# A state-space block followed by an attention block on one core: the first batch's last norm, the key loads and the value projection are put in other places

## The chip, the cores and the metric

The kernel runs on one core of a Trainium2 chip. The core has five engines that run side by side, each taking its instructions in order: TensorE (PE) for matrix products, VectorE (DVE), ScalarE (ACT), GpSimd (POOL), and SyncE (SP), which here issues all DMA transfers. They wait for each other through semaphores. SBUF is the on-chip memory of 128 partitions; PSUM, eight banks of 2 KB per partition, takes what TensorE produces. GpSimd reads and writes SBUF, not PSUM, in this kernel.

The metric is the device time of one execution in microseconds (us).

## The reference

Two layers, for 2 batches of 2048 rows of 512 features, in float32:

```python
# layer 0: modulation by a condition vector, an S5 scan, a feed-forward part
y_mod = _ln(y) * (1 + scale_a[:, None]) + shift_a[:, None]
a_y = _s5(y_mod, ...)                      # complex diagonal recurrence along the rows
y = y + gate_a[:, None] * a_y
y_mod = (_ln(y) * (1 + scale_c) + shift_c) * (1 + scale_ff) + shift_ff
y = y + gate_ff[:, None] * (gelu(y_mod @ W1 + b1) @ W2 + b2)
# layer 1: attention with 16 heads of 32 features, a norm before and after
h = _sln(hidden, w, ...)                   # gamma * layernorm + beta, from the condition
q, k, v = split(h @ Wqkv.T + bqkv)
att = softmax(q @ k.T) / D ** 0.5
out = (att @ v) @ Wp.T + bp
h1 = out + hidden
return _sln(h1, w, ...) + h1
```

The last line is the "last norm" of the title: mean and variance of each row of `h1`, then a product with a row `g` of 512 values, plus a row `t`, plus `h1` itself.

## The kernel before

**First part, about 1380 us.** Each batch is cut into four chunks of 512 rows, eight in all (`order`). While one chunk goes through the feed-forward part, the next one is prepared and the one before is turned into keys, queries and values: `at_norm` (statistics, normalisation, the additions of the bias row on GpSimd, one write of the rows to DRAM as `x2`), `at_features` (transposes), `at_heads` (keys and queries, written as `kd`, `qd`), `at_values` (values, written as `vd`). What is left of this for the last two chunks stands in the list `left` and runs at the *seam*, while the attention starts. There `ones` has a single PSUM bank, so that each product must be emptied before the next one can start.

**Second part, the attention.** A *block* is one batch, one pair of heads and 512 queries: 2 x 8 x 4 = 64 blocks (`blocks`; the order of the last eight is changed). Each block takes NP = 8 *periods*; the main loop over `j` writes one period per round. Below, "period 5" is a round with `j` mod 8 = 5. For each block the 2048 keys are 16 tiles of 128, and the kernel works on two blocks at once:

- For the block AHEAD = 15 periods later it finds each query's maximum: `keep` computes the scores of tiles 0 to 9, copies them to SBUF with ScalarE and keeps a running maximum on VectorE (`run`; the first tile has none, and it falls in period 1); `across` computes the scores of tiles 10 to 15 the other way round (`m`) and reduces them on VectorE (`top`). Periods 0 and 4 keep two tiles, the others one.
- `turn_run` (periods 2 and 4) transposes the running maximum; `spread` (period 5) sends the negated maxima through DRAM (`flat`) back as a tile `shift` over all partitions.
- For the current block, `take_off` adds `shift` to kept tiles on GpSimd, one period before they are used and from period 7 of the block before on; `make` computes tiles 10 to 15 again and adds `shift` on VectorE (`pT`); ScalarE takes the exponentials; `weighted` multiplies with the values one period later.

Scores (`s`) have two PSUM tiles of two banks, `m` one of two banks, the output `o` one bank, and one bank, tag `pt`, is shared by `turn_run`, `spread`, the rows of the last norm, and the last norm's own tiles.

**Loads.** `load_k` loads the keys of a pair of heads with eight transfers of 256 KB, once every four blocks; `load_q` the queries of a block with eight of 64 KB, in period 3; `load_v` the values of a pair with two.

**The closing.** When a batch's heads are done, each tile of 128 queries (`qt`, 16 per batch) is *closed*: `fetch` (six transfers: the outputs, the divisors `by`, the rows `xr`), `divide` (GpSimd), `project` (product with `Wp`, one of its four groups per period for batch 0), `moments` (VectorE), `deviation` (VectorE: the inverse root by Newton steps on columns of one value per partition), `last_norm` (ScalarE, then the product with `g` on VectorE), `close` (GpSimd adds `t` and the rest; a write of the result). The 16 tiles of batch 0 are closed during the blocks of batch 1, in 16 of the blocks 34 to 57, those of batch 1 near the end.

The order is written out by hand: `after(j, what, ...)` puts a step at the start of period `j`, ahead of what the loop itself issues there, in the order in which the steps are listed. No scheduler moves anything. For batch 0's tile `qt`:

```python
k = NP * (NPAIR * NQ * (b + 1) + 2 + 3 * qt // 2) + 3
for g in range(NG):
    after(k + 3 + g, project, b, qt, (g,))
last = k + 6
after(k, fetch, b, qt)
after(k + 2, divide, b, qt)
after(last + 1, deviation, b, qt)
after(last + 2, last_norm, b, qt)
after(last + 3, close, b, qt)
```

In the loop, a period issues in this order: the steps that are due, `make`, `across`, the first exponential, `keep`, the pieces of `left`, the second exponential, `take_off`, `weighted`.

Of the kernel before, what the change touches and what calls it, by code (L numbers as in the profile page):

```python
# [19 lines left out]
P = 128  # L20
# [19 lines left out]
def tile_s5_block_then_sln_attention(  # L40
# [497 lines left out]
        nc.sync.dma_start(dst[0, g * P : (g + 1) * P, at], hi.bitcast(F32))  # L538
        nc.sync.dma_start(dst[1, g * P : (g + 1) * P, at], lo.bitcast(F32))

    def at_values(b, c, t):
        pv = ones.tile([P, CH], F32, name="pv")
        for k in range(KC):
            nc.tensor.matmul(
                pv, fts[b, c][:, k, t * P : (t + 1) * P], wv[:, k, :], start=k == 0, stop=k == KC - 1
            )
        vt = work1.tile([P, D], F32, name="vt", tag="gated")
        nc.vector.tensor_add(vt, pv, bv_row)
        nc.sync.dma_start(vd[b][c * CH + t * P : c * CH + (t + 1) * P, :], vt)


# [129 lines left out]
    left = []  # L681
    for chunk in order[-2:]:
        for t in range(TT):
            left.append((at_values, *chunk, t))
    for j in range(2 * KC):
        left.insert(TT + j, (at_heads, *order[-1], j))
    for k in range(KC):
# [206 lines left out]
    def project(b, qt, groups=tuple(range(NG))):  # L894

        o4, h, *py = held[b, qt]
        if py:
            py = py[0]
        elif len(groups) == NG:
            py = ps.tile([P, 2, CH], F32, name="py2", tag="m")[:, 0, :]  # L900
        else:
            py = ps.tile([P, CH], F32, name="py", tag="pt")
        for g in groups:
            nc.tensor.matmul(py, o4[:, g, :], wp[:, g, :], start=g == 0, stop=g == NG - 1)
        held[b, qt] = o4, h, py
        if groups[-1] == NG - 1:
            held[b, qt] = h, moments(h, py)

    def moments(h, py):
        nc.vector.tensor_add(h, py, h)  # L910
# [4 lines left out]
        return mv  # L915

    def deviation(b, qt):

        h, mv = held[b, qt]
        w = ps.tile([P, 3], F32, name="dev", tag="pt")  # L920
        v, c = w[:, 0:1], w[:, 1:2]
        half = small.tile([P, 1], F32, name="half3")
        y = small.tile([P, 1], F32, name="scale3", bufs=3)
        nc.vector.tensor_scalar(v, mv[:, 1:2], EPS, None, ALU.add)
        nc.vector.tensor_scalar(half, v, -0.5, None, ALU.mult)
        nc.vector.tensor_scalar(
            y.bitcast(I32), v.bitcast(I32), -0.5, float(0x5F3759DF), ALU.mult, ALU.add
        )
        for _ in range(3):
            nc.vector.tensor_scalar(c, y, y, half, ALU.mult, ALU.mult)  # L930
            nc.vector.scalar_tensor_tensor(y, c, 1.5, y, ALU.add, ALU.mult)
        shift = small.tile([P, 1], F32, name="shift3", bufs=3)
        nc.vector.tensor_scalar(c, mv[:, 0:1], y, None, ALU.mult)
        nc.vector.tensor_scalar(shift, c, -1.0, None, ALU.mult)
        held[b, qt] = h, y, shift

    def last_norm(b, qt):

        h, scale, shift = held[b, qt]
        z = ps.tile([P, CH], F32, name="z", tag="pt")  # L940
        nc.scalar.activation(z, h, AF.Identity, bias=shift, scale=scale)
        y = work.tile([P, D], F32, name="y")
        nc.vector.tensor_tensor(y, z, ending[b][0], ALU.mult)  # L943
        held[b, qt] = h, y

    def close(b, qt):

        h, y = held.pop((b, qt))
        nc.gpsimd.tensor_tensor(h, h, ending[b][1], ALU.add)  # L949
        nc.gpsimd.tensor_tensor(y, y, h, ALU.add)  # L950
        nc.sync.dma_start(out[b, qt * P : (qt + 1) * P, :], y)


# [98 lines left out]
    due = {}  # L1052

    def after(j, what, *args):
        due.setdefault(j, []).append((what, args))

    N = len(blocks)
    FIRST = -AHEAD - 8
    OPEN = -4
    for i, n in enumerate(opens):  # L1060
        free = NP * (max(m for m in range(N) if pair_of[m] == i - 2) + 1) if i > 1 else FIRST
        after(max(free, NP * n - AHEAD - 12), load_k, i)
        after(max(OPEN, NP * n - 9), load_v, i)
    for n in range(N):
        after(max(FIRST + 1 + n, NP * n - AHEAD - 6), load_q, n)
        after(NP * n - AHEAD + NP + 1, turn_run, n, 0)
# [2 lines left out]
    for b in range(NB):  # L1069
        for c in range(NQ):  # L1070
            j = NP * (blocks.index((b, NPAIR - 1, c)) + 1) + 1
            if (b, c) == (LB, LC):
                most = slice(0, NH - 4)
                j = NP * (N - 1) - 2
                after(j - 3, fetch_sums, b, c, most)
                after(j - 1, invert, b, c, most)
                after(j + 1, end_fetch)
                after(NP * (N - 1) + 3, end_fetch_more)
                for g in range(NG - 1):
                    after(j + 5 + g, end_divide, g)  # L1080
                after(NP * N + 2, end_project, list(range(NG - 1)))
                after(NP * N + 20, end_last)
                continue
            after(j, fetch_sums, b, c)
            after(j + 2, invert, b, c)
            if c == 0:
                after(j + 2, last_rows, b) if b == LB else after(NP * (NPAIR * NQ * (b + 1) + 2), last_rows, b)
            for t in range(TT):
                qt = c * TT + t
                if b == LB:  # L1090
                    k = j + 3 + 2 * t
                    after(k + 3, project, b, qt)
                else:

                    k = NP * (NPAIR * NQ * (b + 1) + 2 + 3 * qt // 2) + 3
                    for g in range(NG):
                        after(k + 3 + g, project, b, qt, (g,))
                last = k + 3 if b == LB else k + 6
                after(k, fetch, b, qt)
                after(k + 2, divide, b, qt)  # L1100
                after(last + 1, deviation, b, qt)
                after(last + 2, last_norm, b, qt)
                after(last + 3, close, b, qt)

    def run_due(j):
        for what, args in due.pop(j, ()):
# [6 lines left out]
    for j in range(FIRST, NP * N + 2):  # L1113
        if j == OPEN:
            assert not left
            late.close()
            fixed = ctx.enter_context(tc.tile_pool(name="fixed", bufs=1))
            kpools.append(ctx.enter_context(tc.tile_pool(name="kpool1", bufs=2)))
            ppool = ctx.enter_context(tc.tile_pool(name="ppool", bufs=2))
            rows = ctx.enter_context(tc.tile_pool(name="rows", bufs=2))  # L1120
            work = ctx.enter_context(tc.tile_pool(name="work2", bufs=2))
            ps_o = ctx.enter_context(tc.tile_pool(name="ps_o", bufs=1, space=PSUM))
            vst = [fixed.tile([P, NKT, 3, HD], F32, name=f"v{i}") for i in range(2)]
            for v in vst:
# [97 lines left out]
```

## Time and profile before

| | us |
|---|---|
| median of 3 runs | 3556.82 (3556.46 to 3561.1) |
| profiled execution, its own time | 3553.08 |
| its span | 3551.2 |
| PE busy | 3375.1 (95%) |
| DVE busy | 2243.7 (63%) |
| ACT busy | 1897.9 (53%) |
| POOL busy | 1977.0 (56%) |
| attention, batch 0 alone (2000 to 2520): PE busy | 507.12 of 520 |
| attention with closings of batch 0 (2600 to 3000): PE busy | 374.86 of 400 |

The profile is of one execution. "Busy" is the time in which an engine had an instruction; matrix products are pipelined, so a busy PE is not one at its peak. PEld is TensorE's weight load, which runs beside its products. In a line of the timeline the first number is the start in us from the beginning of the span, the second the duration, then the engine, the line of the kernel, the operation, the tiles written and read with their shapes, and in brackets the idle time of the engine just before, with what ended it. "SPq" is the queue that issues transfers. "x4" means four instructions of the kind in a row.

### The profile page before, as it was taken

The numbers are of one execution on the slowest core, as the hardware profiler recorded it, in microseconds if no ns is written. First come the engines' busy times: TensorE is split into PE (matmuls) and PEld (weight loads), VectorE is DVE, ScalarE is ACT, GpSimd is POOL, SyncE is SP. The second block draws the span as 40 slices with busy tenths as digits, with TensorE's granted clock in tenths as the row PEclk, the third lists the DMA queues.
The fourth block names the chain that finished last, engine by engine and source line by source line (L and its number), as shares of the span: only waits on it lengthen the run. The fifth ranks groups of instructions, "written<-read, shape, count | busy, mean of one in ns | idle before, by whom it ended". The sixth has DMA issues, their size and how long they took to land. (4 is left out here: it accounts for less than half of the span.)

```text
span 3551.2 us, 34223 instructions
## 1 busy us (share of the span) xinstructions
PE 3375.1 (95%) x11752; PEld 1531.9 (43%) x11752; DVE 2243.7 (63%) x3184; ACT 1897.9 (53%) x2143; POOL 1977.0 (56%) x1000
## 2 busy tenths in 40 slices
PE   7999999999999998899999999999999999999986
PEld 4444444444444443444444444444444444444432
DVE  6233232323222212589999999898888888988875
ACT  2111112111111111488888888888777877877853
POOL 4223131313131311288778888887777777777875
PEclk8999999999999999999999999999999999999998
DMA  8011111111101112412321222232323323323233
GB/s 296 1 36 39 45 42 48 36 48 36 54 33 39 36 45 74 119 47 64 76 69 49 71 65 70 49 75 61 87 67 81 82 69 77 76 72 88 59 94 98
DMA packets 201710, 237.07 MB, mean 67 GB/s; under 512 B 89857, under 2 KB 119041, under 8 KB 197441
## 3 DMA queue, kind: packets, MB, share of 16 engines
q1 hardware_dynamic: 201536, 234.89, 23.8%
q8 instruction: 93, 1.52, 0.2%
q14 instruction: 81, 0.66, 0.1%
HBM read 166.91 MB, written 67.76 MB: 66 GB/s over the span
## 5 line engine op out<-in xcount | busy, mean ns | idle before, releaser
L810 POOL TENSOR_TENSOR x<-x,shift 128x1024 f32<-128x1024 f32 x640 | 1505.1, 2391 | 284.1 <-DMA shift<-flat 237.6
L762 ACT COPY x<-s 128x1024 f32<-128x1024 f32 x640 | 635.2, 1013 | 297.7 <-PE s L751 294.2
L751 PE MATMUL s<-qs,ks 128*128 128x512 f32 x2048 | 699.5, 433 | 78.0 <-DVE run L767 55.9
L821 ACT ACTIVATE x<-x 128x1024 f32<-128x1024 f32 x640 | 676.4, 1057 | 42.8 <-POOL x L810 42.7
L767 DVE TENSOR_TENSOR run<-s,run 128x1024 f32<-128x1024 f32 x512 | 625.2, 1221 | 76.3 <-ACT x L762 57.4
L831 PE MATMUL o<-x,v 128*64 128x512 f32 x2560 | 669.5, 618 | 0.9 <-ACT x L821 0.9
L816 DVE TENSOR_TENSOR pT<-s,shift 128x1024 f32<-128x1024 f32 x384 | 467.4, 1217 | 49.8 <-PE s L751 44.2
L781 DVE TENSOR_REDUCE top<-m 128x1 f32<-128x768 f32 x512 | 485.9, 949 | 19.6 <-PE m L776 19.2
L751 PEld LDWEIGHTS s<-qs,ks 128*128 128x128 f32 x2048 | 347.4, 190 | 333.3 <-DVE run L767 144.7
L502 PE MATMUL po<-w_sb,hid 128*128 128x512 f32 x1024 | 460.3, 592 | 0.0
L489 PE MATMUL ph<-fT,w_sb 128*128 128x512 f32 x1024 | 459.7, 593 | 0.0
L821 ACT ACTIVATE pT<-pT 128x1024 f32<-128x1024 f32 x384 | 407.5, 1061 | 76.6 <-DVE pT L816 63.2
L493 ACT ACTIVATE hid<-ph,vec 128x512 f32<-128x512 f32 x128 | 88.0, 687 | 591.4 <-PE ph L489 591.4
L831 PE MATMUL o<-pT,v 128*64 128x512 f32 x1536 | 397.3, 596 | 4.6 <-ACT pT L821 4.6
L160 DVE SCALAR_TENSOR_TENSOR lo<-pk,vec,hi 128x512 fp32r<-128x512 f32 x64 | 48.0, 751 | 501.5 <-ACT hi L159 501.5
L776 PE MATMUL m<-ks,qs 128*128 128x384 f32 x1024 | 288.0, 362 | 7.0 <-DVE top L781 3.3
L489 PEld LDWEIGHTS ph<-fT,w_sb 128*128 128x128 f32 x1024 | 191.8, 190 | 226.5 <-issue 226.5
L502 PEld LDWEIGHTS po<-w_sb,hid 128*128 128x128 f32 x1024 | 191.1, 190 | 221.5 <-issue 221.5
L436 POOL TENSOR_TENSOR m<-m,m 128x512 f32<-128x512 f32 x8 | 13.1, 1643 | 442.1 <-DVE m L434 442.1
L159 ACT ACTIVATE hi<-pk,vec 128x512 fp32r<-128x512 f32 x64 | 44.0, 688 | 391.9 <-PE pk L532 391.9
L831 PEld LDWEIGHTS o<-x,v 128*64 128x64 f32 x2560 | 139.5, 136 | 263.6 <-issue 157.9
L512 POOL TENSOR_TENSOR x<-x,gated 128x512 f32<-128x512 f32 x32 | 39.6, 1271 | 349.5 <-DVE gated L511 349.5
(236 smaller groups left out, 2825.1 us busy)
## 6 DMA issues: line engine op xcount, KB each, us to landing
ks<-kd SPq DMA_DIRECT2D x128, 256.0 KB
qs<-qd SPq DMA_DIRECT2D x512, 64.0 KB
shift<-flat SPq DMA_DIRECT2D x64, 512.0 KB
x<-in_x SPq DMA_DIRECT2D x8, 1024.0 KB
w_sb<-in_w SPq DMA_DIRECT2D x8, 1024.0 KB
x<-x SPq DMA_DIRECT2D x8, 1024.0 KB
kd<-hi SPq DMA_DIRECT2D x32, 256.0 KB
kd<-lo SPq DMA_DIRECT2D x32, 256.0 KB
```

Of the source, the lines that this page charges most:

```text
L489: nc.tensor.matmul(ph, w1_sb[:, k, f * P : (f + 1) * P], fts[b, c][:, k, :], start=k == 0, stop=k == KC - 1)
L493: nc.scalar.activation(hids[f], ph, AF.Gelu_apprx_tanh, bias=vec[:, V_B1 + f : V_B1 + f + 1], scale=1.0)
L502: nc.tensor.matmul(pos[b, c][:, t, :], hid[:, t * P : (t + 1) * P], w2_sb[:, f, :], start=f == 0, stop=f == FC - 1,)
L751: nc.tensor.matmul(s[:, e, :], kst[pair_of[n], e][:, kt * P : (kt + 1) * P], qst[n][:, e, :], start=True, stop=True,)
L762: nc.scalar.copy(x, s)
L767: nc.vector.tensor_tensor(runs[n], s, kept[n, 0] if kt == 1 else runs[n], ALU.max)
L776: nc.tensor.matmul(m[:, i, :YW], qst[n][:, e, t * P : (t + 1) * P], kst[pair_of[n], e][:, k : k + YW], start=True, stop=True,)
L781: nc.vector.tensor_reduce(tops[n][:, j, 0:1], m[:, :, :YW], AX.XY, ALU.max, negate=True)
L810: nc.gpsimd.tensor_tensor(x, x, shifts[n], ALU.add)
L816: nc.vector.tensor_tensor(x, s, shifts[n], ALU.add)
L821: nc.scalar.activation(x, x, AF.Exp)
L831: nc.tensor.matmul(outs[n][64 * e : 64 * e + 64, :], v[:, kt, e : e + 2, :], x[:, e, :], start=first, stop=final,)
```

## The change

Five things, in the order of the code:

1. `at_values` gets a flag. With it, ScalarE copies the product from PSUM to SBUF and GpSimd adds the bias row there; without it, VectorE does both as before. It is set for the last chunk but one.
2. At the seam, the pieces of `left` in period -16 (the four `at_values` of the last chunk but one) are written ahead of `at_norm` of the last chunk, not behind it.
3. `moments` is a step of its own. For batch 0, `moments` and `deviation` go to the end of their period (`closing`, carried out behind the second exponential), not to its start.
4. The columns of `deviation` lie in SBUF (before: `v` and `c` in PSUM, bank `pt`); the second instruction of a Newton step is a `tensor_scalar` with the column as pointer, and one instruction makes `shift` where there were two. For batch 0, ScalarE writes the norm into SBUF, GpSimd multiplies with `g`, and `add_t` puts `h + t` into the tile that held the outputs; `fetch` comes two periods earlier, `last_norm` two and `close` three periods later.
5. `load_k` comes five periods later (period 2, before: period 5; the first one at -22 instead of -23), and the first `load_v` at -2 instead of -4.

```diff
-    def at_values(b, c, t):
+    def at_values(b, c, t, beside_norm=False):
...
-        nc.vector.tensor_add(vt, pv, bv_row)
+        if beside_norm:
+            nc.scalar.copy(vt, pv)
+            nc.gpsimd.tensor_tensor(vt, vt, bv_row, ALU.add)
+        else:
+            nc.vector.tensor_add(vt, pv, bv_row)
...
-            left.append((at_values, *chunk, t))
+            left.append((at_values, *chunk, t, chunk != order[-1]))
...
+    def add_t(b, qt):
+        h, ht, *_ = held[b, qt]
+        nc.gpsimd.tensor_tensor(ht, h, ending[b][1], ALU.add)
 
     def deviation(b, qt):
 
-        h, mv = held[b, qt]
-        w = ps.tile([P, 3], F32, name="dev", tag="pt")
-        v, c = w[:, 0:1], w[:, 1:2]
-        half = small.tile([P, 1], F32, name="half3")
+        h, ht, mv = held[b, qt]
+        v = small.tile([P, 1], F32, name="v3")
+        c = small.tile([P, 1], F32, name="c3")
         y = small.tile([P, 1], F32, name="scale3", bufs=3)
+        shift = small.tile([P, 1], F32, name="shift3", bufs=3)
         nc.vector.tensor_scalar(v, mv[:, 1:2], EPS, None, ALU.add)
-        nc.vector.tensor_scalar(half, v, -0.5, None, ALU.mult)
         nc.vector.tensor_scalar(
             y.bitcast(I32), v.bitcast(I32), -0.5, float(0x5F3759DF), ALU.mult, ALU.add
         )
+        nc.vector.tensor_scalar(v, v, -0.5, None, ALU.mult)
         for _ in range(3):
-            nc.vector.tensor_scalar(c, y, y, half, ALU.mult, ALU.mult)
-            nc.vector.scalar_tensor_tensor(y, c, 1.5, y, ALU.add, ALU.mult)
-        shift = small.tile([P, 1], F32, name="shift3", bufs=3)
-        nc.vector.tensor_scalar(c, mv[:, 0:1], y, None, ALU.mult)
-        nc.vector.tensor_scalar(shift, c, -1.0, None, ALU.mult)
+            nc.vector.tensor_scalar(c, y, y, v, ALU.mult, ALU.mult)
+            nc.vector.tensor_scalar(y, c, 1.5, y, ALU.add, ALU.mult)
+        nc.vector.tensor_scalar(shift, mv[:, 0:1], -1.0, y, ALU.mult, ALU.mult)
...
-        z = ps.tile([P, CH], F32, name="z", tag="pt")
-        nc.scalar.activation(z, h, AF.Identity, bias=shift, scale=scale)
...
-        nc.vector.tensor_tensor(y, z, ending[b][0], ALU.mult)
+        if b == LB:
+            z = ps.tile([P, CH], F32, name="z", tag="pt")
+            nc.scalar.activation(z, h, AF.Identity, bias=shift, scale=scale)
+            nc.vector.tensor_tensor(y, z, ending[b][0], ALU.mult)
+        else:
+            nc.scalar.activation(y, h, AF.Identity, bias=shift, scale=scale)
...
-        nc.gpsimd.tensor_tensor(h, h, ending[b][1], ALU.add)
-        nc.gpsimd.tensor_tensor(y, y, h, ALU.add)
+        if b == LB:
+            ht = h
+            nc.gpsimd.tensor_tensor(h, h, ending[b][1], ALU.add)
+        else:
+            nc.gpsimd.tensor_tensor(y, y, ending[b][0], ALU.mult)
+        nc.gpsimd.tensor_tensor(y, y, ht, ALU.add)
...
-        after(max(free, NP * n - AHEAD - 12), load_k, i)
-        after(max(OPEN, NP * n - 9), load_v, i)
+        after(max(free, NP * n - AHEAD - 7) if i > 1 else max(FIRST, NP * n - AHEAD - 7), load_k, i)
+        after(max(OPEN + 2, NP * n - 9), load_v, i)
...
+                    closing(k + 6, moments, b, qt)
                 last = k + 3 if b == LB else k + 6
-                after(k, fetch, b, qt)
+                after(k if b == LB else k - 2, fetch, b, qt)
                 after(k + 2, divide, b, qt)
-                after(last + 1, deviation, b, qt)
-                after(last + 2, last_norm, b, qt)
-                after(last + 3, close, b, qt)
+                (after if b == LB else closing)(last + 1, deviation, b, qt)
+                after(last + (2 if b == LB else 4), last_norm, b, qt)
+                after(last + (3 if b == LB else 6), close, b, qt)
+                if b != LB:
+                    after(last + 4, add_t, b, qt)
...
         if j == -AHEAD - 1:
-            at_norm(*order[-1])
             pieces = TT
...
             what(*args)
+        if j == -AHEAD - 1:
+            at_norm(*order[-1])
         if now is not None:
             exponentials(now, uses[k][1])
+        run_due(j + 0.5)
```

More of the change, by code (lines that the diff above doesn't have):

```diff
@@ L905, in project, with moments @@
         held[b, qt] = o4, h, py
-        if groups[-1] == NG - 1:
-            held[b, qt] = h, moments(h, py)
-    def moments(h, py):
+    def moments(b, qt):
+        o4, h, py = held[b, qt]
         nc.vector.tensor_add(h, py, h)
@@ L914, in moments @@
         nc.vector.bn_aggr(mv, st)
-        return mv
+        held[b, qt] = h, o4.rearrange("p g q -> p (g q)"), mv
+    def add_t(b, qt):
+        h, ht, *_ = held[b, qt]
+        nc.gpsimd.tensor_tensor(ht, h, ending[b][1], ALU.add)
     def deviation(b, qt):
-        h, mv = held[b, qt]
-        w = ps.tile([P, 3], F32, name="dev", tag="pt")
-        v, c = w[:, 0:1], w[:, 1:2]
-        half = small.tile([P, 1], F32, name="half3")
+        h, ht, mv = held[b, qt]
+        v = small.tile([P, 1], F32, name="v3")
+        c = small.tile([P, 1], F32, name="c3")
         y = small.tile([P, 1], F32, name="scale3", bufs=3)
+        shift = small.tile([P, 1], F32, name="shift3", bufs=3)
         nc.vector.tensor_scalar(v, mv[:, 1:2], EPS, None, ALU.add)
-        nc.vector.tensor_scalar(half, v, -0.5, None, ALU.mult)
         nc.vector.tensor_scalar(
@@ L928, in deviation @@
         )
+        nc.vector.tensor_scalar(v, v, -0.5, None, ALU.mult)
         for _ in range(3):
-            nc.vector.tensor_scalar(c, y, y, half, ALU.mult, ALU.mult)
-            nc.vector.scalar_tensor_tensor(y, c, 1.5, y, ALU.add, ALU.mult)
-        shift = small.tile([P, 1], F32, name="shift3", bufs=3)
-        nc.vector.tensor_scalar(c, mv[:, 0:1], y, None, ALU.mult)
-        nc.vector.tensor_scalar(shift, c, -1.0, None, ALU.mult)
-        held[b, qt] = h, y, shift
+            nc.vector.tensor_scalar(c, y, y, v, ALU.mult, ALU.mult)
+            nc.vector.tensor_scalar(y, c, 1.5, y, ALU.add, ALU.mult)
+        nc.vector.tensor_scalar(shift, mv[:, 0:1], -1.0, y, ALU.mult, ALU.mult)
+        held[b, qt] = h, ht, y, shift
     def last_norm(b, qt):
-        h, scale, shift = held[b, qt]
-        z = ps.tile([P, CH], F32, name="z", tag="pt")
-        nc.scalar.activation(z, h, AF.Identity, bias=shift, scale=scale)
+        h, ht, scale, shift = held[b, qt]
         y = work.tile([P, D], F32, name="y")
-        nc.vector.tensor_tensor(y, z, ending[b][0], ALU.mult)
-        held[b, qt] = h, y
-    def close(b, qt):
-        h, y = held.pop((b, qt))
-        nc.gpsimd.tensor_tensor(h, h, ending[b][1], ALU.add)
-        nc.gpsimd.tensor_tensor(y, y, h, ALU.add)
+        if b == LB:
[4 more added lines that the diff above has]
+            nc.scalar.activation(y, h, AF.Identity, bias=shift, scale=scale)
+        held[b, qt] = h, ht, y
+    def close(b, qt):
+        h, ht, y = held.pop((b, qt))
+        if b == LB:
[4 more added lines that the diff above has]
+        nc.gpsimd.tensor_tensor(y, y, ht, ALU.add)
         nc.sync.dma_start(out[b, qt * P : (qt + 1) * P, :], y)
@@ L1055, in after, with closing @@
         due.setdefault(j, []).append((what, args))
+    def closing(j, what, *args):
+        due.setdefault(j + 0.5, []).append((what, args))
     N = len(blocks)
@@ L1092, in tile_s5_block_then_sln_attention @@
                     after(k + 3, project, b, qt)
+                    after(k + 3, moments, b, qt)
                 else:
```

## The prediction

> **What bounds the kernel now.** The table of waits says who waits for whom, but its sums mix stages. I therefore read busy times by stage, and marked in the timeline each period's first matmul on `m` (L776), which cuts the attention into periods. In the columns below, "x" counts instructions; after the engines come the granted clock, the DMA share and GB/s. The first row is a block of batch 0, the second a block of batch 1 with one closing of batch 0.
>
> ```profile
> core 0: us, PE busy (x) PEld busy (x) DVE busy (x) ACT busy (x) POOL busy (x), PEclk, DMA share, GB/s
> 2390.77:2419.55 28.78, 28.24 (x123) 12.84 (x122) 26.36 (x28) 25.71 (x29) 23.71 (x11) 1.00 0.16 44
> 2620.06:2654.23 34.17, 32.07 (x130) 14.20 (x129) 30.05 (x42) 26.74 (x30) 27.23 (x14) 1.00 0.37 81
> ```
>
> An undisturbed block takes 28.8 us with TensorE (PE) busy 98%. Its eight intervals, from period 1 to 2 on, are 4.25, 3.35, 3.20, 4.00, 3.87, 3.35, 2.78, 4.01 us. The 27 blocks from 2419.55 take 120 us more than that, and the excess repeats to 0.02 us: each closing's four matmul groups add 0.85, 0.86, 0.56 and 1.05 (3.32, PE's own work), its deviation, norm and close -0.51, 1.56, 0.87, 0.14 (2.06). Five times the third of these is some 1.5 larger, at half clock. The rest is late shifts.
>
> Before the attention comes the seam (timeline):
>
> ```profile
> 1380.57 3.60 PE L544 MATMUL pv<-wv,fT 128*128 128x512 f32 x8
> 1390.79 3.81 DVE L143 TENSOR_SCALAR xn<-x,mean,rstd 128x512 f32<-128x512 f32 x4
> 1394.52 0.68 DVE L548 TENSOR_TENSOR vt<-pv,bv_row 128x512 f32<-128x512 f32 x1
> 1395.26 5.51 PE L544 MATMUL pv<-wv,fT 128*128 128x512 f32 x8 [11.09 <-DVE vt L548]
> 1409.17 0.91 PE L776 MATMUL m<-ks,qs 128*128 128x384 f32 x2
> ```
>
> The first `pv` is done at 1384.2, but VectorE (DVE) empties it only after `at_norm`'s whole statistics and normalisation. PE stands 11.1 us and then runs eight matmuls at two thirds of its clock (5.51 us for 3.60).
>
> Late shifts, an undisturbed one first (timeline):
>
> ```profile
> 2405.70 0.27 SPq L802 DMA_DIRECT2D flat<-neg_row  x1
> 2410.82 2.40 POOL L810 TENSOR_TENSOR x<-x,shift 128x1024 f32<-128x1024 f32 x1 [5.07 <-DMA shift<-flat]
> ...
> 2434.48 0.27 SPq L802 DMA_DIRECT2D flat<-neg_row  x1
> 2440.41 0.35 SPq L804 DMA_DIRECT2D shift<-flat  x1
> 2444.35 11.72 POOL L810 TENSOR_TENSOR x<-x,shift 128x1024 f32<-128x1024 f32 x5 [10.01 <-DMA shift<-flat]
> 2450.04 1.06 PE L751 MATMUL s<-qs,ks 128*128 128x512 f32 x2 [2.29 <-DVE run L767]
> ```
>
> GpSimd (POOL) can start 5.1 us after `flat` is issued, but 9.9 us when `load_k`'s eight transfers (from 2428.4) were issued in the same period 5.
>
> A closing (timeline):
>
> ```profile
> 2654.10 0.68 DVE L910 TENSOR_TENSOR xr<-py,xr 128x512 f32<-128x512 f32 x1
> 2655.65 1.21 DVE L816 TENSOR_TENSOR pT<-s,shift 128x1024 f32<-128x1024 f32 x1
> 2658.43 0.16 DVE L924 TENSOR_SCALAR dev<-mv 128x1 f32<-128x1 f32 x1
> 2660.66 0.16 DVE L934 TENSOR_SCALAR shift<-dev 128x1 f32<-128x1 f32 x1
> 2662.01 0.74 PE L751 MATMUL s<-qs,ks 128*128 128x512 f32 x2 [1.20 <-DVE pT L816]
> 2663.87 0.68 DVE L943 TENSOR_TENSOR y<-z,g_row 128x512 f32<-128x512 f32 x1
> 2670.53 0.73 PE L751 MATMUL s<-qs,ks 128*128 128x512 f32 x2
> ```
>
> DVE runs without a gap from 2654.10 to 2671.72, and PE waits for it.
>
> **The Trainium skill.** "SBUF — State Buffer", section "Who interferes with whom", says that DVE and GpSimd share one port pair under an exclusive lock: a DVE instruction with two SBUF inputs, or in a two-port mode, waits out a GpSimd one. "VectorE: DVE Perf Modes", section "What auto-detection actually checks", gives that mode to an SBUF-to-SBUF instruction with one source whose outermost sizes are even or equal; a column of one element might count. The trace agrees on wide tiles, not on a column (timeline):
>
> ```profile
> 158.39 1.71 POOL L462 TENSOR_TENSOR xn<-xn,r_scale 128x512 f32<-128x512 f32 x1
> 159.01 0.21 DVE L454 COPY last<-m 128x1 f32<-128x1 f32 x2
> ...
> 3540.36 1.73 DVE L1026 TENSOR_TENSOR o<-o,h 128x512 f32<-128x512 f32 x1 [1.16 <-POOL h L1024]
> ```
>
> The last takes 0.69 without GpSimd; the column copies don't wait for the 1.71. "TensorE: Matmul & The Clock Gate", Part 1, lets idle windows halve the clock; here it was 0.60 in 2525.5 to 2529.6, after waits.
>
> **The change part by part.**
>
> *Values at the seam.* The four `at_values` now precede `at_norm`, with ScalarE emptying PSUM (a 128x512 copy: 0.59, from `raw`). Before, `pv` starts 4.49 apart (1401.55, 1406.04); with the shorter copy 4.4. The second pays some 1.1 more, because the first copy's buffer is held by GpSimd's third `gated` addition (to 1385.3). So `m` starts at 1380.57 + 3 x 4.4 + 1.1 + 3.2 = 1398.1 instead of 1409.17: -11. `at_norm` ends on DVE at 1394.6, hidden behind these matmuls. On GpSimd the four additions of `bv_row` (1.27 each) come ahead of `at_norm`'s; on SP the four `vd` writes come ahead of the `x2` write, to about 1405, before the heads' writes behind it. If these writes were held up: at most 5. I take -10.8.
>
> *First v load.* It moves behind the first shift on SP. That shift needed 8.3 us from `flat` (1480.00 to 1488.28); at 5.2 GpSimd is done with its first tile at 1487.6, then the table load (to 1488.6) decides: the first exponential at 1488.65 instead of 1490.67, -2.0. `v` is issued some 4 us later and first needed some 12 us after that; if it doesn't land in time, up to +3.
>
> *Keys.* Issued in period 2, three periods (10.6 us) ahead of the next `flat`; the transfers take some 10. The first use stays seven periods (25 us) away. They pass `load_q` (period 3) on SP, whose queries are needed later. Six blocks of batch 1 lose: 3.30, 5.65, 5.00, 1.37, 3.49, 4.67, sum 23.5. In batch 0 the same lateness (up to 7.8 us from `flat`) cost PE nothing, so 2 us of remaining overlap cost nothing either. I take -23.5; bounds -25 and -12.
>
> *Closings of batch 0, 16 times.* Removed from DVE: the product with g (0.60 until the next starts). Deviation: 2.31 from 2658.43 to `pT`. After: ten instructions; a plain one is spaced 0.19, one pointer adds 0.06 (L933: 222 against 158 ns), two 0.12 (L930: 281). So 4 x 0.19 + 0.06 (shift) + 3 x (0.32 + 0.25) = 2.5. The moments (1.55) stood in a gap that the last `py` group makes; now they follow period 1's `top`, where an undisturbed block has a gap of 1.28 (no running maximum in that period), but `pT` starts only at 2654.44, when its `s` is there. DVE's chain then ends at 2654.44 + (17.62 - 1.55 - 2.31 - 0.60 + 1.55 + 2.5) = 2671.65 against 2671.72. The wait moves: `py` keeps the bank that the transposes of the running maximum need until 2657.2 (0.25), and late is not the third scores tile but the `m` of period 4, behind `top` (1.7). I take -0.07 x 16 = -1, bounds -16 and +10. Longer single waits may bring two more half-clock spells: +2.
> ScalarE gains nothing: the norm moves to period 5, where it idles 0.66 for 0.80 of work. GpSimd's product is 1.28 more per closing, in period 7; there it waits 1.5 to 2.9 us for the shift anyway, and no longer stands 5 us for z; without that cover 20. `fetch` two periods earlier (six DMAs, past `load_q`) ends GpSimd's waits for `by` (43 us), which were hidden.
>
> *Batch 1's deviation*, 12 times 0.2 us longer but out of the shared bank: 0, bounds -3 and +3.
>
> Sum: -10.8 - 2.0 - 23.5 - 1 + 2 = -35.3. The profiled execution took 3553.1 (span 3551.2), 3.7 below the median of the runs; 3556.8 - 35.3 = **3521.5**.
>
> **Rivals.** *Keys only half freed* (chance 0.15): the burst with the queries behind it still reaches `flat`; half the 23.5 remains: 3533. For it: 2.5 MB in 11 us. Against: a late shift up to 7.8 us was free. *The closings' wait vanishes* (0.17): PE's own outputs of the previous period cover the deviation, 1.5 of the 2.06 goes: 3521.5 - 23 - 3 = 3496. Against: DVE has no gap there. *Columns take the port lock* (0.05), the case that ends slower: each of ten column instructions waits out a 2.39 us GpSimd tile, on average half, 12 us a closing, 28 closings: some 3850. It decides from 35/28 = 1.3 us per closing. Against: the column copies above.
>
> **How the numbers follow.** The forecast's case has 0.63. Its own range, from seam (2), keys (4) and closings (10), is 3509 to 3534; with the rivals at 3496 and 3533, 3495 to 3536. A measurement here tells 0.2% (7 us) from no change: faster 0.93, same 0.02, slower 0.05.
>
> **What would show it.** `m` first at about 1398; 5.1 us from `flat` to GpSimd in every fourth block; closings still adding some 5.3 us, with PE waiting at period 4's `m`; column instructions at 0.15 to 0.28 us. Wrong if these stretch, or if late shifts stay.

## The result and the profile after

The changed kernel takes 3513.66 us (median of 4 runs, 3509.6 to 3514.7). The kernel before took 3556.64 beside it. The ratio is 0.9878, with a 95% interval of 0.9861 to 0.9895. The profiled execution went from 3553.08 to 3509.6, -43.5 us, where the forecast had -35.3. The sum came out 8 us off, but two of its terms were wrong by more than that, in opposite directions.

Marking each period's first matmul on `m` again (now L780) cuts both executions into the same stages:

| us | before | after | difference |
|---|---|---|---|
| seam: first `pv` to first `m` | 28.60 | 17.35 | -11.25 |
| first `m` to the third block (`j` = 17) | 146.27 | 146.40 | +0.13 |
| batch 0's blocks, `j` = 17 to 257 | 864.11 | 863.87 | -0.24 |
| blocks with batch 0's closings, `j` = 257 to 473 | 898.07 | 869.97 | -28.10 |
| `j` = 481 to the end | 204.77 | 200.49 | -4.28 |

The busy times of an undisturbed block and of a block with one closing, after the change (columns as in the forecast's first view):

```profile
core 0: us, PE busy (x) PEld busy (x) DVE busy (x) ACT busy (x) POOL busy (x), PEclk, DMA share, GB/s
2379.67:2408.47 28.80, 28.27 (x123) 12.85 (x121) 26.38 (x28) 25.71 (x29) 23.50 (x11) 1.00 0.14 44
2501.51:2535.28 33.77, 32.21 (x131) 14.29 (x130) 29.43 (x39) 26.64 (x30) 29.24 (x15) 1.00 0.25 67
```

An undisturbed block is what it was. The block with a closing takes 5.0 us more: 3.31 for the four matmul groups, which is PE's own work, and 1.65 for the rest of the closing (before 2.06).

The seam (timeline):

```profile
1385.57 0.59 ACT L549 COPY vt<-pv 128x512 f32<-128x512 f32 x1 [10.64 <-POOL x L512]
...
1398.20 0.91 PE L780 MATMUL m<-ks,qs 128*128 128x384 f32 x2
...
1416.98 0.75 DVE L160 SCALAR_TENSOR_TENSOR lo<-pk,vec,hi 128x512 fp32r<-128x512 f32 x1 [5.58 <-DMA kd<-lo]
```

ScalarE empties the first `pv` as soon as GpSimd has released the buffer, PE no longer stands 11 us behind `at_norm`, and the products come 4.4 us apart (5.4 the first time). `m` starts at 1398.20, where the forecast had 1398.1. The last line is the price. On SP the write of `x2` waits for the norm until 1405.72, and the eight query transfers behind it go right ahead of the heads' first write. That write, issued at 1411.73, takes 5 us to land, and its tile can be rewritten only then. Period -12 is 1.06 longer for it (0.4 to 1.4 in the nine kernels here that have this seam).

A closing (timeline):

```profile
2643.32 0.15 DVE L932 TENSOR_SCALAR v<-mv 128x1 f32<-128x1 f32 x1
...
2643.48 4.70 POOL L814 TENSOR_TENSOR x<-x,shift 128x1024 f32<-128x1024 f32 x2
...
2643.88 0.27 DVE L938 TENSOR_SCALAR c<-scale,v 128x1 f32<-128x1 f32 x1
...
2645.68 1.22 DVE L820 TENSOR_TENSOR pT<-s,shift 128x1024 f32<-128x1024 f32 x1
...
2647.82 0.62 PE L780 MATMUL m<-ks,qs 128*128 128x384 f32 x2 [1.17 <-DVE top L785]
```

The ten column instructions take 2.36 us from 2643.32 to the next `pT`. GpSimd works on two tiles all that time, and none of the ten is stretched (0.15, 0.21 or 0.27 us by the number of columns that an instruction takes as pointers). PE now waits once, at the `m` of period 4. Before, it waited 1.20 at `s` behind `pT` (the prediction shows that line) and two us later 0.51 behind `run` (timeline of the kernel before):

```profile
2664.01 0.73 PE L751 MATMUL s<-qs,ks 128*128 128x512 f32 x2 [0.51 <-DVE run L767]
```

The late shifts are not gone. In block 37 (timeline; "SPq" issues transfers in order):

```profile
2570.26 1.22 SPq L890 DMA_DIRECT2D xr<-x  x1
2571.52 7.77 SPq L733 DMA_DIRECT2D ks<-kd  x8
2580.34 8.10 SPq L743 DMA_DIRECT2D qs<-qd  x8
2588.53 0.27 SPq L806 DMA_DIRECT2D flat<-neg_row  x1
...
2594.28 11.64 POOL L814 TENSOR_TENSOR x<-x,shift 128x1024 f32<-128x1024 f32 x5 [10.32 <-DMA shift<-flat]
...
2599.93 0.74 PE L755 MATMUL s<-qs,ks 128*128 128x512 f32 x2 [2.39 <-DVE run L771]
```

`neg_row`, which `flat` sends, is ready at 2580.63 (ScalarE's copy, 2580.39 to 2580.63). `flat` is issued at 2588.53, 7.9 us later, because SP has still to issue the queries. Those take 3.6 to 3.9 us for eight transfers when little is under way (before, at 2588.56 and 2552.57), and 8.1 here, behind 2 MB of keys, which themselves took 7.8 behind the six transfers of `fetch`. From `flat` to GpSimd it is 5.75 us (5.1 undisturbed), so the transfer itself is hardly late. In block 33, which has keys and no fetch, the queries take 8.4 us too, but begin five us after the keys, and `flat` goes out only 0.7 us late. In the five blocks where keys and fetch meet (37, 41, 49, 53, 56) `flat` goes out 5.9 to 7.9 us late, and the end of the block and the start of the next lose 4.35, 1.05, 2.56, 1.34 and 0.46 us, 9.8 in all. Before, it was 23.5 in six other blocks.

### The profile page after: what moved, and what is told of

Read it like the earlier page. It is cut to its first block, busy times and chain, and to the rows that moved or that the text cites. A ratio compares the mean times of both kernels' runs of the same rounds, so it can differ in the third digit from the quotient of the medians.

```text
span 3507.7 us, 34138 instructions
## 1 busy us (share of the span) xinstructions
PE 3362.0 (96%) x11752; PEld 1526.4 (44%) x11752; DVE 2229.1 (64%) x3136; ACT 1897.0 (54%) x2147; POOL 1997.6 (57%) x1020
## 5 line engine op out<-in xcount | busy, mean ns | idle before, releaser
L780 PE MATMUL m<-ks,qs 128*128 128x384 f32 x1024 | 284.8, 359 | 23.7 <-DVE top L785 22.1
```

The source lines that it names most:

```text
L780: nc.tensor.matmul(m[:, i, :YW], qst[n][:, e, t * P : (t + 1) * P], kst[pair_of[n], e][:, k : k + YW], start=True, stop=True,)
```

## The experiments

Each kernel is compared with the kernel before, which took 3555.6, 3556.8 and 3557.9 us in the three groups. The stage "closings' blocks" is `j` = 257 to 473 of the profiled execution. What a block or a closing "loses" or "costs" is the sum of what its periods took over those of an undisturbed block; a closing's matmul groups are left out. A "spell" is a stretch at half clock in a closing. A late shift is named by the block in which its `flat` is issued.

### Which part brings what: three parts alone

**Seam alone**: `at_values` ahead of `at_norm` with ScalarE and GpSimd, and the first `load_v` at `OPEN + 2`.

> The kernel before with the seam alone changed (values ahead of the norm, emptied by ScalarE; first load of v two periods later). Theory of the forecast: the first m at about 1398.1 instead of 1409.2 and period 0 two us shorter, together -12.8 us, so 3544. What the traces of the two kernels suggest: -10.9 at the first m, +1.0 lost again some three periods later, -2.0 in period 0, +1.0 in period 1 where the values now come late: -10.9 in all, 3546. In both the later blocks stay as they were before.

Measured 3538.84, ratio 0.996 (0.9945 to 0.9975). The stage from `pv` to `m` is 17.35 and the next one 146.48, just as in the changed kernel: -11 us from the seam. Periods -1 to 1, around the first use of `v`, take 14.68 and not 15.63. Up to `j` = 17 this comes to 11 us, but the medians differ by 16.8. In the profiled executions the rest lies in the closings' blocks, whose code is the same: 889.94 us against 898.07, with 2 spells against 5 and 19.7 us of late shifts against 23.5. So much can differ there with nothing changed in the stage; whether by chance or by the earlier start was not shown.

**Keys alone**:

```diff
-        after(max(free, NP * n - AHEAD - 12), load_k, i)
+        after(max(free, NP * n - AHEAD - 7) if i > 1 else max(FIRST, NP * n - AHEAD - 7), load_k, i)
```

> The kernel before with the loads of the keys alone moved to period 2. Theory of the forecast (the late shifts were the keys' transfers, and they are gone): -23.5 us, 3533. Theory from the trace after (the eight key transfers fill SP's queue; the queries behind them are issued in 8 us and not in 4, and flat, which is behind the queries, goes out late where the six transfers of fetch come in the same block): the six old stalls go, new ones of 1 to 3 us each come at the end of blocks 37, 41, 49, 53 and 56, so -10 to -17, 3540 to 3547. Here fetch is still in period 3, behind the queries, so the new stalls may be longer than in the changed kernel.

Measured 3557.16, ratio 1.0011 (1.0003 to 1.0018); closings' blocks 904.75, 6.7 more than before. Both theories fall. All six old stalls are gone, as both had said. But blocks 37, 41, 49, 53 and 56 lose 8.3, 4.5, 8.2, 5.2 and 5.1 us in periods 5 and 6, at a place that neither had named. There PE waits for the first group of `py`, by 6.17 us in block 37. It waits for GpSimd's division, and the division for `by` (timeline). `fetch` is still in period 3 and stands behind keys and queries.

```profile
2605.94 1.26 POOL L891 TENSOR_TENSOR o<-o,by 128x512 f32<-128x512 f32 x1 [13.16 <-DMA by<-invd]
...
2607.25 2.08 PE L904 MATMUL py<-wp,o 128*128 128x512 f32 x2 [6.17 <-POOL o L891]
```

**Closings alone**: items 3 and 4 of the change, `fetch` and `close` included, with seam and keys as before.

> The kernel before with the closings alone changed (moments and deviation at the end of their periods, columns in SBUF, product with g on GpSimd, fetch two periods earlier); keys and seam as before. Theory of the forecast: -1 from VectorE's chain and +2 from spells of half clock, so no change, 3557 to 3558. Theory from the trace after: 1.65 us a closing instead of 2.06, 16 times, -6.6; and the five closings that lost 1.5 more at half clock lose it no longer, -7: 3543. The late shifts of the keys stay in both, and with fetch earlier they may even be shorter.

Measured 3526.79, ratio 0.9925 (0.991 to 0.994): -29 us, twice what I expected. The closings' blocks take 867.70, which is 2.3 *less* than in the changed kernel with its moved keys. Each closing costs 1.65, none runs at half clock, and with the keys still in period 5 the late shifts shrank from 23.5 to some 8 us. So something in the closings' part frees the shifts, and no gain in this stage is left for the move of the keys. The 2.3 us themselves say little, since late shifts differ by more than that between executions (19.7 and 23.5 above).

### What in the closings' part freed the shifts

**Fetch alone, two periods earlier, in the kernel before**:

```diff
-                after(k, fetch, b, qt)
+                after(k if b == LB else k - 2, fetch, b, qt)
```

> The kernel before with one step alone moved: fetch of batch 0's tiles two periods earlier (period 1 and not 3). Theory of SP's queue: before, the fetch of period 3 stands right ahead of the keys of period 5 and of flat; ahead of them by four periods, it no longer does, and most of the late shifts go although the keys stay in their place: -12 to -16 of the 23.5 us, and with fewer long waits also some half-clock spells of 1.5 each: 3535 to 3543. Theory of the forecast (the fetch is hidden, the late shifts are the keys' alone): no change, 3555.

Measured 3552.64, ratio 0.9987 (0.9979 to 0.9996). My theory falls: blocks 32, 36, 40, 44, 48 and 52 still lose 3.1, 6.1, 4.2, 1.4, 5.7 and 4.1 us at their end and the start of the next block, 24.6 in all, as before. In block 40 the last of the keys are still issued just ahead of `flat`, and `shift` follows `flat` by 8.2 us (7.4 in the kernel before).

**Close alone, three periods later, in the kernel before**:

```diff
-                after(last + 3, close, b, qt)
+                after(last + (3 if b == LB else 6), close, b, qt)
```

> The kernel before with one step alone moved: close of batch 0's tiles three periods later (period 7 and not 4), fetch and keys in their old places. Theory of SP's queue, second form: the write of the result, which waits on SP for GpSimd's sums in period 4, holds the keys behind it until some 4 us before flat; without it in front they go 7 us earlier, and the late shifts of blocks 36, 44 and 48 (5.65, 1.37 and 3.49) go, those of 32, 40 and 52 stay: -9 to -10.5, 3546. Rival (the moved close does nothing for SP; the late shifts shrank by less work on VectorE): no change, 3556.

Measured 3549.04, ratio 0.9971 (0.9961 to 0.9982). Blocks 36 and 48 lose nothing any more and block 44 0.26; 32, 40 and 52 still lose 3.5, 5.1 and 6.6. The timeline of SP in block 36, first of the kernel before:

```profile
2552.57 3.86 SPq L739 DMA_DIRECT2D qs<-qd  x8
2563.63 0.36 SPq L951 DMA_DIRECT2D out<-y  x1
2564.03 3.68 SPq L729 DMA_DIRECT2D ks<-kd  x8
2568.26 0.27 SPq L802 DMA_DIRECT2D flat<-neg_row  x1
2576.05 0.34 SPq L804 DMA_DIRECT2D shift<-flat  x1
```

and of the kernel with the later close:

```profile
2557.03 3.90 SPq L739 DMA_DIRECT2D qs<-qd  x8
2560.97 3.67 SPq L729 DMA_DIRECT2D ks<-kd  x8
2572.70 0.27 SPq L802 DMA_DIRECT2D flat<-neg_row  x1
2573.97 0.34 SPq L804 DMA_DIRECT2D shift<-flat  x1
```

In the kernel before, the write of the result stands ahead of the keys in SP's order and waits for GpSimd's sums until 2563.63, with SP idle for seven us. The keys are ready to go all that time, and when they go they are 4.2 us ahead of `flat`. Without the write in front they follow the queries at once, 11.7 us ahead of `flat`, and `shift` follows `flat` by 1.3 us and not by 7.8. In these blocks it was a *waiting* transfer on SP that brought the keys so close to `flat`. Blocks 40 and 52 have no `close`. They lose 5.1 and 6.6 here, 4.2 and 4.1 with `fetch` alone moved, and 1.7 and 2.0 with the whole closings' part; what does that was not taken apart.

### The fetch in the changed kernel, and the keys at a better place

**Fetch back to period 3 in the changed kernel** (the diff of the fetch above, reversed):

> The changed kernel with fetch alone back in its old place (period 3, behind the queries). Theory: as in the kernel with the keys alone moved, the fetch stands behind the keys and the queries in blocks 37, 41, 49, 53 and 56, the division comes late, and the first group of the product waits in TensorE's order: 4 to 8 us each, less the 10 us of late shifts that go with it, +20 to +25: 3534 to 3539. Theory of the forecast (fetch is hidden wherever it stands): 3514.

Measured 3535.53, ratio 0.9938 (0.9918 to 0.9957), as the theory said; closings' blocks 896.11, 26.1 more. Block 37 in the timeline:

```profile
2570.06 8.49 SPq L743 DMA_DIRECT2D qs<-qd  x8
2578.59 0.42 SPq L882 DMA_DIRECT2D o<-od  x1
2579.06 1.93 SPq L886 DMA_DIRECT2D by<-invd  x4
...
2587.38 1.26 POOL L895 TENSOR_TENSOR o<-o,by 128x512 f32<-128x512 f32 x1 [11.92 <-DMA by<-invd]
...
2588.69 2.08 PE L908 MATMUL py<-wp,o 128*128 128x512 f32 x2 [6.32 <-POOL o L895]
```

The division waits 11.9 us for the divisors, and PE then 6.3 for the division. So the earlier fetch, worth at most some 4 us alone, is what makes the keys in period 2 bearable.

**Keys in period 6 in the changed kernel**, behind `flat` and `shift`:

```diff
-        after(max(free, NP * n - AHEAD - 7) if i > 1 else max(FIRST, NP * n - AHEAD - 7), load_k, i)
+        after((max(free, NP * n - AHEAD - 11) if i > 1 else NP * n - AHEAD - 11) if i else FIRST + 1, load_k, i)
```

> The changed kernel with the loads of the keys moved once more, to period 6, so that they are issued behind flat and shift and not ahead of them. Theory of SP's queue: in no block does flat stand behind the keys; the stalls at the end of blocks 37, 41, 49, 53 and 56 (2.67, 0.65, 2.15, 0.93, 0.05, with 1.68, 0.40, 0.41, 0.41, 0.40 at the start of the block behind each) are gone, -9 to -10 us: 3504. Rival, the bandwidth of the transfers: 2 MB right behind the shift delay the shift itself as they did before the change (9.9 us from flat to GpSimd), and the time goes back towards 3535.

Measured 3503.79, ratio 0.9859 (0.9844 to 0.9874); closings' blocks 860.07, 9.9 less than the changed kernel. No late shift is left in this stage, and the rival falls. SP around block 37 (timeline):

```profile
2558.80 0.34 SPq L808 DMA_DIRECT2D shift<-flat  x1
2559.19 4.54 SPq L733 DMA_DIRECT2D ks<-kd  x8
...
2575.71 7.94 SPq L743 DMA_DIRECT2D qs<-qd  x8
2585.78 0.27 SPq L806 DMA_DIRECT2D flat<-neg_row  x1
```

The keys go right behind the shift, which they delay by about a us (GpSimd starts 4.7 us after its issue, 3.6 where no keys follow). They have a whole block before the next `flat`. The queries still take 7.9 us to issue here, now behind `fetch` alone, but `flat` gets through in time.

### Inside a closing

The next three take the kernel with keys in period 6 as their base (3503.79; 1.65 us a closing, no late shifts), since nothing else disturbs the closings there.

**Moments back at the start of their period**: `after(k + 6, moments, b, qt)` for `closing(k + 6, moments, b, qt)`.

> The changed kernel with the keys in period 6, and the moments back at the start of their period (ahead of pT), all the rest of the closing as changed. Theory of the forecast (VectorE runs without a gap from pT on, and only the sum of its work counts): 17.07 us from the moments to the end of the chain against 16.87 from pT, so the closings cost about 1.5 to 1.65 us each as with the moments at the end: 3502 to 3504. Rival (the place is what helped: moments ahead of pT hold two tiles of scores and make two waits 2 us apart, and those bring the clock down): 2.06 a closing and some spells of 1.5: 3510 to 3518.

Measured 3498.42, ratio 0.9835 (0.9809 to 0.9861): 1.40 a closing, no spells. The stage takes 856.26, 3.8 less than the base, so the end of the period costs 0.25 each. Of this, 0.16 is the later start of the transposes, which wait there for the bank that `py` holds, as the forecast had it (0.25). The rival falls: it is not the moments' place that brought the two waits.

**The product with `g` back on VectorE**, from PSUM, in period 5:

```diff
-        if b == LB:
-            z = ps.tile([P, CH], F32, name="z", tag="pt")
-            nc.scalar.activation(z, h, AF.Identity, bias=shift, scale=scale)
-            nc.vector.tensor_tensor(y, z, ending[b][0], ALU.mult)
-        else:
-            nc.scalar.activation(y, h, AF.Identity, bias=shift, scale=scale)
+        z = ps.tile([P, CH], F32, name="z", tag="pt")
+        nc.scalar.activation(z, h, AF.Identity, bias=shift, scale=scale)
+        nc.vector.tensor_tensor(y, z, ending[b][0], ALU.mult)
...
-        else:
-            nc.gpsimd.tensor_tensor(y, y, ending[b][0], ALU.mult)
```

> The changed kernel with the keys in period 6, and the product with g back on VectorE, from PSUM, in period 5; GpSimd has 1.28 us less in period 7. Theory of the forecast (GpSimd's product is hidden, VectorE's 0.60 is on the path): +0.6 a closing, +9.6, 3513. Rival (in period 5 VectorE has caught up and waits for TensorE): nothing, 3504. If GpSimd's product in period 7 costs time in the changed kernel, this one is faster than 3504.

Measured 3510.11, ratio 0.9868 (0.9845 to 0.9891). The closings' blocks take 863.88, 3.8 more, and not 9.6. In the eight blocks that also hold the next tile's `py` groups it costs nothing, since VectorE waits for PE there; in the other eight it costs 0.41 (0.75 in one). GpSimd's product in period 7 is hidden, as forecast.

**The deviation back at the start of its period**, ahead of `pT`, with the columns in SBUF as changed:

```diff
-                (after if b == LB else closing)(last + 1, deviation, b, qt)
+                after(last + 1, deviation, b, qt)
```

> The changed kernel with the keys in period 6, and the deviation back at the start of period 2, ahead of pT; moments at the end of period 1, all the rest as changed. Theory (the spells of half clock came from two waits some 2 us apart, 1.20 at s behind pT and 0.51 behind run, which the deviation ahead of pT makes): the two waits are back, and with them spells of 1.5 in some of the 16 closings; 1.5 to 2.0 a closing, and 3504 to 3515. Rival (the spells came from the bank of the columns or from the longer waits for shifts): no spells, 3502 to 3506.

Measured 3520.45, ratio 0.9895 (0.9875 to 0.9915), 5 us above my range; closings' blocks 875.35, 15.3 more than the base. Each closing costs 2.09 again (+0.45, 7.1 in all), and five of the 16 run 1.6 longer at half clock (8.2). Two closings of this kernel, the first with a spell and the second without (windows, columns as above), and then PE at the first of them (timeline).

```profile
2609.00:2613.00 4.00, 3.22 (x8) 1.25 (x10) 4.00 (x5) 2.69 (x3) 1.40 (x3) 0.79 0.78 158
...
2644.00:2648.00 4.00, 2.42 (x8) 1.09 (x10) 4.00 (x5) 2.24 (x3) 4.00 (x3) 1.00 0.00 0
```

```profile
2609.14 0.73 PE L755 MATMUL s<-qs,ks 128*128 128x512 f32 x2 [1.20 <-DVE pT L820]
2610.01 0.62 PE L780 MATMUL m<-ks,qs 128*128 128x384 f32 x2
2611.14 1.09 PE L755 MATMUL s<-qs,ks 128*128 128x512 f32 x2 [0.51 <-DVE run L771]
```

Both closings have the same pair of waits, 1.20 and 0.51 two us apart, yet only the first loses its clock (0.79, and 0.78 in the four us behind). The bank of the columns is not needed for it, since they lie in SBUF here.

Why it strikes five of 16, the traces show. In each kernel the record of the granted clock has half-clock stretches in the attention that begin on a grid of 3.413 us. In this kernel's closings they begin at 2611.32, 2710.30, 2809.29, 2908.28 and 3007.26, which is 98.98 or 98.99 apart, 29 steps of the grid, and each lasts one step. Six of the kernels have the pair, in 96 closings. It takes 3.2 us from the start of the first wait to the end of the second. Where it began between 0.65 us before and 0.56 us behind a point of the grid, so that it lay nearly whole in one step, a spell followed: 24 times. Where it began anywhere else none did: 72 times. And in the six kernels whose closings have the single wait of 1.17, none of 96 has a spell, wherever on the grid the wait fell. So the pair is the cause, and the place where it falls decides. "TensorE: Matmul & The Clock Gate", Part 1, of the Trainium skill says that activity is counted in free-running windows of about 3.4 us, and the grid agrees with it. A spell's cost agrees too: one such window at half speed would lose 1.7 (an estimate from that page), and 1.6 to 1.7 were measured here.

### Two faster versions

**The deviation's columns on GpSimd**, keys in period 6:

```diff
-        nc.vector.tensor_scalar(v, mv[:, 1:2], EPS, None, ALU.add)
+        on = nc.vector if b == LB else nc.gpsimd
+        on.tensor_scalar(v, mv[:, 1:2], EPS, None, ALU.add)
...
-                (after if b == LB else closing)(last + 1, deviation, b, qt)
-                after(last + (2 if b == LB else 4), last_norm, b, qt)
+                after(last + (1 if b == LB else 3), deviation, b, qt)
+                after(last + (2 if b == LB else 5), last_norm, b, qt)
```

> The changed kernel with the keys in period 6, batch 0's ten column instructions of the deviation on GpSimd in period 4, and the last norm in period 6. GpSimd idles 4.7 us there until the norm comes. Theory (the closings' 1.65 us are VectorE's lack of a gap, and the 2.36 us of columns are more than that): if a column takes GpSimd 0.2 to 0.4 us, the waits at period 4's m go, -1.5 x 16 = -24: 3480. Rival (columns take GpSimd over 0.5 us each, so that its first tile of the next period is late and ScalarE waits for it): no gain, or slower than 3504.

Measured 3473.81, ratio 0.9767 (0.9751 to 0.9784), 30 us under the base; closings' blocks 830.09. The costliest of the column instructions on GpSimd (groups by line, of the blocks with closings; busy us, mean ns, idle before):

```profile
L939 POOL TENSOR_SCALAR c<-scale,v 128x1 f32<-128x1 f32 x48 | 16.4, 341 | 5.1
```

A column takes GpSimd 0.19 to 0.34 us and the ten 3.55 with the gaps, against 2.36 on VectorE. But GpSimd stood idle there. PE's waits in the closings' blocks, in the base and then in this kernel (table of waits: total, times, longest):

```profile
PE m L780 <- DVE top L785: 18.7, 16, 1.2
PE s L755 <- DVE run L771: 10.1, 40, 0.7
```

```profile
PE s L755 <- DVE run L771: 10.9, 41, 0.7
```

The 16 waits at `m` are gone, and a closing no longer costs anything beyond its matmul groups (-0.27, and 1.65 in the base).

**With the moments at the start, and the first load of v back at -4** (`max(OPEN, NP * n - 9)`):

> The fastest so far (keys in period 6, columns of batch 0 on GpSimd), with the moments back at the start of their period and the first load of v back at -4. Moments: worth 0.24 a closing where the columns were on VectorE, -3.9; where VectorE is no longer late, 0 to -4. First load of v: period 0 two us longer and period 1 one us shorter, +1, if the late values are what cost in period 1; by the forecast +2. Together 3471 to 3475.

Measured 3470.46, ratio 0.9757 (0.9741 to 0.9774), the fastest. The closings' blocks take 826.34, another 3.7 less, so the moments' place still counts. With the first load of v at its old place, periods -1 to 1 take 15.78 us against 14.61. That holds in all kernels: 15.46 to 15.86 in the six that load it at -4, and 13.25 to 14.68 in the eight that load it at -2.

## Why the prediction was right or wrong

**Time and range.** 3521.5 was forecast, 3509 to 3534 in its own case, and 3513.66 came. That it came so near is luck in part: the late shifts gave 9.8 us less than forecast, the spells 9.3 more. By its terms:

| term | forecast | measured |
|---|---|---|
| seam, values | -10.8 | -11.25, and +1.06 in period -12 |
| first v load, periods -1 to 1 | -2.0 | -1.0 (15.63 to 14.59) |
| late shifts | -23.5 | 23.5 to 9.8: -13.7 |
| closings, 16 times | -1 | -6.6 |
| half-clock spells at closings | +2 | -7.3 |
| after `j` = 481 | 0 | -4.3 |

**Seam: right**, by its own steps. What it bounded at 5 ("if these writes were held up") came as 1.06.

**First v load: right in kind, half the size here.** Period 0 is 2.0 shorter, as forecast, and period 1 is 1.0 longer. The loss in period 1 is no fixed price of the edit: with the same code up to there, four of the other kernels take 4.74 to 5.12 in it (5.09 before, 6.08 here). Why it comes in some executions stays open; that `v` lands late in them was not shown.

**Keys: the step that failed.** "They pass `load_q` (period 3) on SP, whose queries are needed later." I asked when the queries are needed, and not what stands behind them in SP's order. That is `flat`, and behind the keys the queries take 8 us to issue and not 3.6. The rival "keys only half freed" had this mechanism ("the burst with the queries behind it still reaches `flat`") and about the right remainder; its time did not come because of the gains elsewhere. The attribution was wrong as well: alone, the move of the keys gains nothing (3557.16), and beside the new closings the stage is no longer with the keys in their old place (867.70 against 869.97). The late shifts shrank with the closings' part, to which the forecast gave none of that gain.

**Fetch: wrong.** It was costed at nothing since GpSimd's waits for `by` "were hidden". They were, before. With the keys in period 2, the earlier fetch is worth 26 us. I had named the cover, but not asked whether the same change takes it away.

**Close: not costed at all.** Three periods later was read as GpSimd work alone. Its `out` transfer, which waits on SP with the keys behind it, was the cause of two of the six late shifts in the kernel before (36 and 48) and of most of a third (44).

**Closings: place right, size off.** PE's wait moved to period 4's `m`, and the transposes wait (0.16, and 0.25 in the forecast). The chain ends 0.42 earlier and not 0.07: the ten columns take 2.36 us, not 2.5, and the rest is 0.2 spread over the chain. The columns take no port lock, so they don't wait for GpSimd: 0.15 to 0.27 us beside a running GpSimd instruction. The doubt that the forecast took from "VectorE: DVE Perf Modes", section "What auto-detection actually checks", of the Trainium skill, does not hold for a column of one element.

**Clock: wrong sign.** "Longer single waits may bring two more half-clock spells." A single wait of 1.17 brought none; the pair did, and moving the deviation to the end of its period removed the pair. The size of this term is chance: the kernel before had 5 spells in its profiled execution, and the four others with moments and deviation in their old places had 2, 4, 2 and 6.

**Tail: open.** -4.3 in these two executions. But over all kernels the tail with the changed columns took 200.5 to 203.8, and with the old ones 201.3 to 204.9, so most of the difference may be chance.

## What to carry to other kernels

On a queue that issues transfers in order, cost a moved transfer by everything behind it: what it must wait for, how long it takes to issue while megabytes are still under way, and which small urgent transfer stands at the end of that line. Here the large load was best right behind the urgent transfer, not ahead of it. And where VectorE had no gap, the chain of tiny instructions was best on an engine that stood idle, though each took longer there. A wait's price also depends on its neighbours: one of 1.2 us cost no clock here, but with another of 0.5 two us later it did whenever the pair fell into one step of the clock's grid.

## What the runs showed that I had not expected

- An SP transfer of the queries is issued in about 0.45 us, and in 0.9 to 1.1 where the keys or a fetch are under way ahead of it: eight in 7.0 to 8.5 and not in 3.6. So the issuing queue itself slows down while large transfers ahead of it are under way; why was not looked into.
- A column instruction on GpSimd takes 0.19 to 0.34 us, against 0.15 to 0.27 on VectorE: here GpSimd is closer to VectorE than on a 128x512 tile with two SBUF inputs (1.28 against 0.69 for the product with `g`, which VectorE reads from PSUM).
- The same code in the closings' blocks took 889.9 and 898.1 us in two executions, since late shifts and spells fell differently. The kernel before went from 3548 to 3564 over all its runs. A difference of a few us between two profiled executions is therefore read here only where the periods show its place.
